# Alternating two accumulation rooms across block boundaries, and a GpSimd power moved one chunk earlier, in a two-layer fp32 network

## The chip, the cores and the metric

The kernel runs on one core of a Trainium2 chip. The metric is the device time of one execution in microseconds (us); lower is better. The kernel before was run three times: 1033.0, 1033.77 and 1033.81 us, median 1033.77.

## The reference, cut to what matters

Two layers follow each other on 2048 rows of 512 numbers. Each layer is an attention and a feed-forward part, and each part is added to its input and layer-normalised. The change lies in the first layer's feed-forward part, whose weights are packed as 4-bit codes with one scale per group of 128 inputs:

```python
w_gu = _dequant_fp4(gate_up_packed, gate_up_scales, 128)   # [2816, 512]
w_down = _dequant_fp4(down_packed, down_scales, 128)       # [512, 1408]
gate_up = jnp.einsum('bsh,oh->bso', x, w_gu)
gate, up = (gate_up[..., :I], gate_up[..., I:])            # I = 1408
h = jax.nn.silu(gate) * up
y = jnp.einsum('bsi,hi->bsh', h, w_down)
rms = jnp.sqrt(jnp.mean(y * y, axis=-1, keepdims=True) + 1e-6)
return y / rms
...
x = _layernorm(x + ffn(x))
```

## The kernel before, in words

**Tiling.** The 2048 rows are four blocks (`NB` = 4) of 512 rows. The hidden width of 1408 is `NI` = 11 chunks of 128. For each block the loop at L625 runs f = 0 to 10; in each pass TensorE computes one chunk of gate and one of up, and the rest of the chip turns them into one chunk of h = silu(gate) * up.

**One chunk.** `scaled_sum` (L452) makes one chunk of gate or of up. For each of the four groups of 128 inputs (k = 0 to 3) TensorE multiplies the unpacked codes with the high and the low part of x (`parts`, the tiles x1Th and x1Tl) into one PSUM bank. The four banks have to be multiplied by their own group scales and added, and that happens in SBUF, in a tile `acc`: for k = 0 ScalarE writes `acc` (L463), for k = 1 to 3 VectorE adds to it (L468; where `by_three` is true the last of them is done by ScalarE and GpSimd, L465 and L466). Banks come from a pool of four (`mm_bank`, L86); chunks with `eight_banks`, which are all of block 0 and f = 9 and 10 of each block, take every second bank from a second pool of four. Then ScalarE applies silu to gate in place (L634) and GpSimd multiplies up and gate into h (L635, called hm in the code).

**The rooms.** `acc` is one of two tiles for gate and one of two for up, allocated at L436 and picked at L454 by `f % 2`. A block has 11 chunks, so f = 10 of one block and f = 0 of the next pick the same room.

**The down projection.** The h of a block is multiplied with the unpacked down weights while the next block's gate and up are made. `down` (L490) is a generator whose steps are single matmuls (L501, L510); the loop takes 5 of them ahead of f = 0 and 8 or 9 after each of f = 0 to 8 (`take`). Its result y lies in one room, `place_w(3, "y")`, which every block uses in turn.

**The work on y.** A finished y is handled one block later still, in blocks 2 and 3 of the loop, by `Normed` (L562): squares of y summed over each row (`squares`, ScalarE, L577, four instructions), the power -0.5 of their mean (`power`, GpSimd, L581 and L582, two instructions on 128x4 numbers), y times that power (`scaled`, ScalarE, L586, four instructions), x + y (`to_x`, GpSimd, L591) and the row statistics and layer norm. `steps` (L600) says after which chunk each of these is issued; L643 calls it.

**Order.** Each engine works through its own queue in order. A planner puts the instructions in that order at build time; it takes an instruction when its inputs are ready by its own reckoning, unless an edge says otherwise. The edges at L636 say that what a pass issues after its chunk comes, on each engine, behind the last gate and up matmul (mm), the last VectorE addition (st), the silu (sl) and the GpSimd product (hm) of that chunk. All waits between engines follow from which instruction reads and writes which tile.

Of the kernel before, what the change touches and what calls it, by code (L numbers as in the profile page):

```python
# [26 lines left out]
NI = I_FF // P  # L27
# [46 lines left out]
def body(ctx: ExitStack, tc: tile.TileContext, a: dict, out: bass.AP):  # L74
# [14 lines left out]
    def acc_bank(name):  # L89
        return pacc.tile([P, 512], F32, tag="acc", name=name)  # L90
# [10 lines left out]
    def place_w(i, name):  # L101
        return wpool.tile([P, KC, C], F32, tag=f"A{i}", name=name)
# [6 lines left out]
    def load_w(dst, name):  # L109
        nc.sync.dma_start(out=dst, in_=a[name].rearrange("(k p) o -> p k o", p=P))  # L110
# [83 lines left out]
    def split_tiles(blk):  # L194

        i, j = ((1, 1), (2, 0), (0, 2), (1, 1))[blk]
        hi = xT_slot(i, "x1Th", F32R)
        lo = wpool.tile([P, KC, 512], F32R, tag=f"A{j}", name="x1Tl")
        return hi, lo

    def split_quarter(parts, blk, i):
        hi, lo = (t[:, :, i * P : (i + 1) * P] for t in parts)
        pt = transposed(x_t[blk][:, i], "x1Tp").rearrange("p (k t) -> p k t", k=KC)
        nc.scalar.copy(hi, pt)  # L204
        nc.vector.tensor_sub(lo, pt, hi.bitcast(F32))
# [66 lines left out]
    for b in range(B):  # L272
        acc = [acc_bank(f"xk{b}_{c}") for c in range(KC)]
# [88 lines left out]
        for n in range(10):  # L362
# [5 lines left out]
            if n >= 1 and n <= 8:  # L368
                i = n - 1
                blk = 2 * b + i // 4  # L370
# [14 lines left out]
            if b == 1 and n in (2, 3, 4, 5):  # L385
                if n == 2:
                    parts = split_tiles(0)
# [23 lines left out]
    def turn(blk, part=range(4)):  # L411

        if 0 in part:
            xT[blk] = xT_tile("x2T")
        for i in part:
            pt = transposed(x_t[blk][:, i], "x2Tp")
            nc.scalar.copy(xT[blk][:, :, i * P : (i + 1) * P], pt.rearrange("p (k t) -> p k t", k=KC))
        return last_turned[0]
# [15 lines left out]
    with tc.tile_pool(name="s2", bufs=1) as wk2:  # L434
        NP = (NI - 1) // 2
        rooms = {n: [wk2.tile([P, 512], F32, name=f"{n}{i}") for i in range(2)] for n in ("gate", "up")}  # L436
# [12 lines left out]
                for j in (slice(0, 3), slice(3, NP)):  # L449
                    yield nc.gpsimd.tensor_sub(dst[:, j], x[:, j], y[:, j])  # L450

        def scaled_sum(f, parts, name, by_three, eight_banks):  # L452

            acc = rooms[name][f % 2]  # L454
            for k in range(KC):
                ps = (acc_bank if eight_banks and k % 2 else mm_bank)(f"{name}p")
                for x in parts:
                    ins = nc.tensor.matmul(  # L458
                        ps, wgu[:, k, f * P : (f + 1) * P], x[:, k], start=x is parts[0], stop=x is parts[1]
                    ).ins  # L460
                s = scale[:, k * FG + f : k * FG + f + 1]
                if k == 0:
                    nc.scalar.activation(acc, ps, AF.Copy, scale=s)  # L463
                elif k == KC - 1 and by_three:
                    nc.scalar.activation(spare, ps, AF.Copy, scale=s)  # L465
                    nc.gpsimd.tensor_add(acc, acc, spare)  # L466
                else:
                    last = nc.vector.scalar_tensor_tensor(acc, ps, s, acc, ALU.mult, ALU.add).ins  # L468
            return acc, ins, last
# [76 lines left out]
        def take(pieces, n):  # L546
            for _ in range(n):
                next(pieces, None)
# [3 lines left out]
        def norm_tiles(blk, mv, part):  # L552

            if blk not in roots:
                rs = roots[blk] = sp.tile([P, 4], F32, tag="rs", name="rs")
                nc.vector.tensor_scalar_add(rs, mv[:, :, 1], 1e-5)
                nc.gpsimd.tensor_tensor(rs, rs, const("mhalf"), ALU.pow)
            for i in part:
                x = x_t[blk][:, i]
                nc.gpsimd.tensor_scalar(x, x, mv[:, i, 0:1], roots[blk][:, i : i + 1], ALU.subtract, ALU.mult)  # L560

        class Normed:  # L562
# [37 lines left out]
            def steps(self):  # L600

                return {
                    0: lambda: self.squares(range(4)),
                    1: lambda: (self.power(), self.scaled(), self.to_x((0, 1))),
                    2: lambda: self.to_x((2, 3)),
                    4: self.stats,
                    5: lambda: self.norm((0,)),
                    7: lambda: self.norm((1,)),
                    8: lambda: self.norm((2, 3)),
                }  # L610
# [12 lines left out]
        for blk in range(NB):  # L623
            h = Hidden(blk)
            for f in range(NI):  # L625
                if f == 0:
                    if blk:
                        with tc.issue_after(mm), tc.issue_after(hm):
                            take(pieces, 5)

                alone = blk == 0 or f >= NI - 2
                gate, mm, st = scaled_sum(f, parts, "gate", False, alone)
                up, mm, st = scaled_sum(NI + f, parts, "up", alone, alone)
                sl = nc.scalar.activation(gate, gate, AF.Silu).ins  # L634
                hm = nc.gpsimd.tensor_mul(h.chunk(f), up, gate).ins  # L635
                with tc.issue_after(mm), tc.issue_after(st), tc.issue_after(hm), tc.issue_after(sl):  # L636
                    if f < NI - 2:
                        take(pieces, 9 if f in (0, NI - 3) else 8)
                    if blk == 0 and f in (2, 4, 6, 8):
                        norm_tiles(3, late, (f // 2 - 1,))  # L640
                    for _ in range((2, 2, 2, 0, 1, 1)[f] if blk == 1 and f < 6 else 0):
                        next(wsums)
                    if blk > 1 and f in old_steps:  # L643
                        old_steps[f]()
                    if f >= NI - 2:
                        if f == NI - 2:
                            if blk < NB - 1:
                                coming = split_tiles(blk + 1)
                            else:
                                Wig = place_w(0, "Wig")  # L650
                                load_w(Wig, "WigT")
                        for i in (0, 1) if f == NI - 2 else (2, 3):
                            if blk < NB - 1:
                                split_quarter(coming, blk + 1, i)
                            else:
                                turn(0, (i,))
            parts = coming
            old, now = now, Normed(blk)
            pieces = down(h, now.room)
            if blk > 0:  # L660
                old_steps = old.steps()
        Wog = place_w(1, "Wog")
        load_w(Wog, "WogT")
        for n, steps in enumerate((11, 12, 10, 12, 10, 10, 14)):
            with tc.issue_after(mm), tc.issue_after(hm):
                take(pieces, steps)
            if n == 0:
                old.squares(range(4))
                old.power()
            if n == 1:  # L670
                for _ in old.rest():
                    pass
            if n < 2:
                turn(1, (2 * n, 2 * n + 1))
            if n == 2:
                lp = logits(0)
# [416 lines left out]
    def finish_ffn(w2, h):  # L1093
# [59 lines left out]
        def steps(b):  # L1153
# [74 lines left out]
            yield  # L1228

        one, two = steps(0), steps(1)  # L1230
        next(one)
        sums_of_h(0, 1)
# [164 lines left out]
```

## Time and profile before

| what | value |
|---|---|
| median of three runs | 1033.77 us |
| the profiled execution: its time, its span | 1033.33 us, 1031.6 us |
| TensorE busy (PE), weight loads (PEld) | 999.9 us (97%), 706.7 us (69%) |
| VectorE (DVE), ScalarE (ACT), GpSimd (POOL) busy | 651.5, 283.9, 306.1 us |
| gate and up of block 0; blocks 1, 2 and 3 begin at about | 255 us; 302, 384 and 471 us |
| mean granted TensorE clock | 0.995 |

The span is the time between the first and the last instruction of the profile; the 1.73 us by which the execution is longer lie around it. [...] idle time of TensorE is read from the gaps between its starts and from the waits, not from the 97%. Weight loads (PEld) run beside the matmuls. In the rows of the timeline, the columns are start and length in us, engine, line, operation, output and inputs, the count of merged instructions, and in square brackets how long the engine was idle before and what released it. In rows of waits the three numbers are us in total, times, and the longest one.

### The profile page before, as it was taken

Reading aid. Unit: us, or ns where it says so; the run is one execution under the profiler, and the core shown is the slowest. Engines: PE = TensorE matmul, PEld = TensorE weight load, DVE = VectorE, ACT = ScalarE, POOL = GpSimd, SP = SyncE. Lnnn points to the kernel's source line nnn. Section 1 sums busy time; section 2 is a strip of 40 time slices with the busy share of each in tenths; the row PEclk is TensorE's granted clock in tenths of the full one; section 3 lists DMA queues with packets and bytes.
Section 4 is the critical chain, followed back from the end, with each engine's and each line's share of the span. In section 5 each row is a group of like instructions: output and inputs, shape, how many; then the busy total and the mean of one; then the engine's idle time right before and its main releaser. Section 6 shows DMA issues by size and latency. Waiting matters only on the chain.

```text
span 1031.6 us, 10932 instructions
## 1 busy us (share of the span) xinstructions
PE 999.9 (97%) x4061; PEld 706.7 (69%) x4061; DVE 651.5 (63%) x1225; ACT 283.9 (28%) x469; POOL 306.1 (30%) x281
## 2 busy tenths in 40 slices
PE   8999999999999998999999999999999999999996
PEld 3454444545767776777778955687687688888885
DVE  1246745376875675675677139446788886689744
ACT  2223232222652244234324043242121123221000
POOL 1100351003785634554556403101005003000022
PEclk9999999999999999999999999999999999999999
DMA  9611123100000000000002050000002422140011
GB/s 346 194 46 56 42 69 98 31 31 0 1 1 1 1 1 0 1 1 1 1 0 93 1 213 1 1 1 1 1 1 82 124 81 82 41 141 24 1 41 41
DMA packets 25688, 48.81 MB, mean 47 GB/s; under 512 B 4652, under 2 KB 6316, under 8 KB 25123
## 3 DMA queue, kind: packets, MB, share of 16 engines
q1 hardware_dynamic: 22995, 42.85, 12.5%
q0 software_dynamic: 1920, 4.22, 1.1%
q10 hardware_dynamic: 720, 1.05, 0.3%
q8 instruction: 32, 0.52, 0.2%
q14 instruction: 21, 0.17, 0.1%
HBM read 39.70 MB, written 10.52 MB: 49 GB/s over the span
## 4 chain that ended last, share of the span: by engine, by line
PE 71%; DVE 10%; issue 9%; ACT 5%; POOL 4%; DMA 0%; POOLq 0%; DVEq 0%; ACTq 0%
PE P L501 11%; PE yp L1141 9%; PE hp L1062 7%; PE qp L210 5%; PE xk L279 5%; PE upp L458 5%; PE ao L210 5%; PE kp L210 4%; DVE gate L468 3%; PE gatep L458 3%; PE ao L945 3%; PE go L901 2%; ACT gate L463 2%; PE kp L296 1%; PE lp L425 1%
## 5 line engine op out<-in xcount | busy, mean ns | idle before, releaser
L468 DVE SCALAR_TENSOR_TENSOR gate<-gatep,scale,gate 128x512 f32<-128x512 f32 x132 | 98.6, 749 | 76.2 <-ACT gate L463 69.8
L174 POOL TENSOR_TENSOR rs<-rs,table 128x4 f32<-128x4 f32 (+1 forms) x21 | 19.6, 936 | 321.2 <-DVE rs L173 320.7
L468 DVE SCALAR_TENSOR_TENSOR up<-upp,scale,up 128x512 f32<-128x512 f32 x115 | 85.9, 747 | 8.1 <-ACT up L463 1.5
L458 PE MATMUL upp<-x1Th,wgu 128*128 128x512 f32 x176 | 75.8, 432 | 10.6 <-ACT gate L463 7.9
L458 PE MATMUL gatep<-x1Th,wgu 128*128 128x512 f32 x176 | 74.5, 430 | 1.2 <-ACT x1Th L204 1.1
L458 PE MATMUL upp<-x1Tl,wgu 128*128 128x512 f32 x176 | 70.5, 403 | 0.0
L458 PE MATMUL gatep<-x1Tl,wgu 128*128 128x512 f32 x176 | 68.6, 399 | 0.1
L635 POOL TENSOR_TENSOR h<-up,gate 128x512 f32<-128x512 f32 x32 | 40.8, 1276 | 87.8 <-DVE up L468 79.7
L501 PE MATMUL P<-wdn,h 128*128 128x256 f32 x256 | 61.9, 379 | 0.0
L458 PEld LDWEIGHTS upp<-x1Th,wgu 128*128 128x128 f32 x176 | 33.6, 191 | 38.2 <-DVE gate L468 18.2
L463 ACT ACTIVATE gate<-gatep,scale 128x512 f32<-128x512 f32 x44 | 30.3, 688 | 104.3 <-PE gatep L458 89.7
L210 PE MATMUL ao<-G,qT 128*128 128x512 f32 x128 | 57.6, 595 | 0.0
L210 PE MATMUL qp<-Wq,x0T 128*128 128x512 f32 x128 | 57.6, 592 | 0.0
L279 PE MATMUL xk<-k,x 128*128 128x512 f32 x128 | 56.7, 592 | 0.0
L945 PE MATMUL ao<-W1o,uT 128*128 128x512 f32 x128 | 55.6, 592 | 0.0
L501 PEld LDWEIGHTS P<-wdn,h 128*128 128x128 f32 x256 | 48.2, 190 | 6.7
L849 POOL TENSOR_TENSOR sum<-sum,sq 128x512 f32<-128x512 f32 x12 | 19.0, 1582 | 107.8 <-issue 84.5
L264 DVE SCALAR_TENSOR_TENSOR k<-kp,e 128x512 f32<-128x512 f32 x16 | 11.0, 691 | 55.4 <-ACT e L263 49.4
L279 PEld LDWEIGHTS xk<-k,x 128*128 128x128 f32 x128 | 24.3, 190 | 30.6 <-issue 29.9
L210 PEld LDWEIGHTS ao<-G,qT 128*128 128x128 f32 x128 | 24.0, 190 | 30.0 <-issue 28.7
L945 PEld LDWEIGHTS ao<-W1o,uT 128*128 128x128 f32 x128 | 24.0, 190 | 28.7 <-issue 28.0
L210 PE MATMUL kp<-Wk,x0T 128*128 128x512 f32 x96 | 43.3, 593 | 0.2 <-DVE k L264 0.2
(335 smaller groups left out, 2131.0 us busy)
## 6 DMA issues: line engine op xcount, KB each, us to landing
pk<-in_gu SPq DMA_DIRECT2D x16, 352.0 KB, 3.8
x<-in_x SPq DMA_DIRECT2D x4, 1024.0 KB, 12.8
w<-in_w SPq DMA_DIRECT2D x1, 4096.0 KB, 14.5
xs<-picked SPq DMA_DIRECT2D x4, 1024.0 KB, 5.0
out<-x SPq DMA_DIRECT2D x4, 1024.0 KB, 4.3
w<-in_w SPq DMA_DIRECT2D x4, 1024.0 KB, 6.4
x0T<-in_xT SPq DMA_DIRECT2D x3, 1024.0 KB, 8.8
pk<-in_dn SPq DMA_DIRECT2D x11, 256.0 KB, 3.5
```

The costliest lines, as they stand in the source:

```text
L174: power = nc.gpsimd.tensor_tensor(rs[:, :n], rs[:, :n], const("mhalf")[:, :n], ALU.pow).ins
L210: nc.tensor.matmul(ps, lhs[:, k], w[:, k], start=start and k == 0, stop=stop and k == KC - 1)
L279: nc.tensor.matmul(acc[c], x_t[2 * b + i // 4][:, i % 4, c * P : (c + 1) * P], k, start=i == 0, stop=i == 7)
L458: ins = nc.tensor.matmul(ps, wgu[:, k, f * P : (f + 1) * P], x[:, k], start=x is parts[0], stop=x is parts[1]).ins
L463: nc.scalar.activation(acc, ps, AF.Copy, scale=s)
L468: last = nc.vector.scalar_tensor_tensor(acc, ps, s, acc, ALU.mult, ALU.add).ins
L501: nc.tensor.matmul(cut, x(j)[:, r], w[:, j], start=j == 0, stop=j == NP - 1 and tail is None)
L635: hm = nc.gpsimd.tensor_mul(h.chunk(f), up, gate).ins
L901: nc.tensor.matmul(ps[:, 256 * m : 256 * m + 256], w[:, k, m], b[:, k, 256 * half : 256 * half + 256], start=k == 0, stop=k == KC - 1,)
L945: nc.tensor.matmul(ao[i], uT[blk][:, k, i * P : (i + 1) * P], W1o[:, k], start=n == 0, stop=n == 3)
L1062: nc.tensor.matmul(ps[:, 256 * j : 256 * j + 256], w[:, k, 2 * g + j], x[:, k], start=k == 0, stop=k == 1)
L1141: nc.tensor.matmul(ps[:, 256 * r : 256 * r + 256], x(r, j), w(j), start=j == 0, stop=j == NJ - 1)
```

## The change

Two edits. First, `scaled_sum` no longer picks its room from f; the caller picks it from the count of chunks over all blocks, `(blk * NI + f) % 2`, the same for gate and up. In block 0 and in block 2 this is the old choice (0 and 22 are even), in blocks 1 and 3 it is the other one. Between f = 10 of a block and f = 0 of the next the room now changes. Nothing else in `scaled_sum` is touched. Second, `power` moves from the step after f = 1 to the step after f = 0, behind `squares`.

```diff
-        def scaled_sum(f, parts, name, by_three, eight_banks):
-
-            acc = rooms[name][f % 2]
+        def scaled_sum(f, parts, acc, name, by_three, eight_banks):
+
             for k in range(KC):
...
-                    0: lambda: self.squares(range(4)),
-                    1: lambda: (self.power(), self.scaled(), self.to_x((0, 1))),
+                    0: lambda: (self.squares(range(4)), self.power()),
+                    1: lambda: (self.scaled(), self.to_x((0, 1))),
                     2: lambda: self.to_x((2, 3)),
...
-                gate, mm, st = scaled_sum(f, parts, "gate", False, alone)
-                up, mm, st = scaled_sum(NI + f, parts, "up", alone, alone)
+                at = (blk * NI + f) % 2
+                gate, mm, st = scaled_sum(f, parts, rooms["gate"][at], "gate", False, alone)
+                up, mm, st = scaled_sum(NI + f, parts, rooms["up"][at], "up", alone, alone)
```

## The prediction, made before the change was run

> **What bounds the kernel now.** I read the page first: the strip of 40 slices, then the shares of the chain that ended last.
>
> ```profile
> PE   8999999999999998999999999999999999999996
> PEclk9999999999999999999999999999999999999999
> ...
> PE 71%; DVE 10%; issue 9%; ACT 5%; POOL 4%; DMA 0%; POOLq 0%; DVEq 0%; ACTq 0%
> ```
>
> TensorE is at work nearly everywhere and carries the chain. So the question is where in the gate and up stage (255 to 560 us) TensorE stands still, and on whom it waits then. The waits of that stretch answer it:
>
> ```profile
> PEld upp L458 <- DVE gate L468: 18.2, 47, 0.9
> PEld upp L458 <- ACT gate L463: 11.3, 8, 3.1
> ...
> ACT y L586 <- POOL ms L582: 9.1, 2, 4.5
> PE upp L458 <- ACT gate L463: 7.9, 8, 2.7
> ```
>
> The first row is a small wait of 47 chunks for a bank, at the pace of VectorE. The second and fourth are the same eight events, few and long: the first up matmul of a chunk waits until ScalarE has written gate and so freed a bank. By the timeline the 7.9 us are twice 2.67 at f = 2 of blocks 2 and 3, 0.89, 0.25 and 0.28 at the three block boundaries, and 1.1 inside block 0, which the change leaves alone. ScalarE in turn waited twice, 4.5 us each, for the power. The chain in order of time shows one of the two, in block 2:
>
> ```profile
> 399.67 1.27 POOL h L635
> 400.94 0.07 issue
> 401.01 0.20 POOL ms L581
> 401.22 0.07 issue
> 401.29 1.04 POOL ms L582
> 402.33 0.02 issue
> 402.36 2.56 ACT y L586 x4
> 404.92 0.58 ACT gate L463
> ...
> 406.33 2.83 PE upp L458 x6
> ```
>
> The product of f = 1, the two power instructions, the four scalings and the gate of f = 2 stand in a row, and TensorE is at its end. Its own timeline says so (bracket: idle before), and the table of windows shows what it does to the clock. The first window is chunk f = 2 of block 1, which has no work on an old y; the second is f = 2 of block 2:
>
> ```profile
> 405.54 0.50 PE L458 MATMUL upp<-x1Th,wgu 128*128 128x512 f32 x1 [2.67 <-ACT gate L463]
> ```
>
> ```profile
> 318.90:326.50 7.60, 7.49 (x33) 5.89 (x32) 4.41 (x6) 2.01 (x3) 4.33 (x4) 1.00 0.01 2
> ...
> 400.70:412.70 12.00, 9.28 (x35) 6.87 (x33) 4.33 (x6) 4.45 (x7) 6.03 (x7) 0.86 0.00 0
> ```
>
> Same matmuls, 12.0 us in place of 7.6, with a granted clock of 0.86 (the number ahead of the two of DMA). The last pair of rows, from the timelines of ScalarE and TensorE, is the boundary between blocks 0 and 1, where the room matters:
>
> ```profile
> 304.41 0.69 ACT L463 ACTIVATE gate<-gatep,scale 128x512 f32<-128x512 f32 x1 [2.73 <-POOL h_even L635]
> ```
>
> ```profile
> 305.15 0.51 PE L458 MATMUL upp<-x1Th,wgu 128*128 128x512 f32 x1 [0.89 <-ACT gate L463]
> ```
>
> Gate of f = 0 waits for the GpSimd product of the old f = 10, which still reads the same room.
>
> [...] after the stall the six up matmuls from 406.33 to 408.95 come every 0.44 us, in a steady chunk every 0.23. [...] 2.67 us without a matmul (3.10 without a weight load) was enough. [...]
>
> **The power, part by part.** Nothing is added; two instructions move up in GpSimd's queue, no DMA and no semaphore of SP is passed. GpSimd's power (0.20 + 1.04 us) now needs the squares of f = 0, which end at 393.5 in block 2; the product of f = 0 ends at 392.9. So it runs from about 393.6 to 394.9. The wait that this adds on GpSimd is 0.7 us; behind it stands only the product of f = 1, whose up is ready at 399.5, so 4.6 us of cover hide it. That hand-over appears at the end of the stage, where power starts 0.08 us after the last squares (601.71 to 601.79).
>
> ScalarE finishes the silu of f = 1 at 397.83, finds the power made, and scales until 400.4 (four at 0.64). Gate of f = 2 is wanted 0.94 us after its first matmul (319.85 against 318.91 in block 1), here at 401.6. So 1.2 us lie between; the stall goes whole. GpSimd's to_x, 2.5 us after the product of f = 1, ends before 403.5, and the next product is due at 407.3 (6.63 after the chunk's start, as in block 1). What is late next in this chunk is the bank wait on VectorE that all chunks have (0.19 + 0.56), and it is within the 7.6.
>
> The gain is the chunk's period. In block 2, first gate matmul of f = 2 to that of f = 3: 412.68 - 400.66 = 12.02; in block 3: 498.81 - 487.05 = 11.76. A steady chunk with the same 8 down matmuls has 7.61 (318.93 to 326.54), and blocks 2 and 3 return to 7.60 at f = 3. Gain 4.41 + 4.15 = 8.56 us. The least is the bare idle time before the matmuls, 2 x 2.67 = 5.3; the rest, 3.2 us, is clock[...]. I take 8.6[...].
>
> **The rooms, part by part.** Block 0 and the inside of each block keep their alternation; f = 0 now takes the room of the old f = 9, whose product ended long ago (300.1 at the first boundary, 380.8 at the second). Gate of f = 0 is then limited by its own matmuls. The weight loads show the high parts of three groups first, then their low parts, the first of which starts at 302.82, 385.21 and 471.56; in a steady chunk ScalarE starts 0.49 us after that matmul (319.36 to 319.85). So gate would start at 303.3, 385.7 and 472.05 instead of 304.41, 386.16 and 472.52. At each boundary I then take the later of two: that bank free 0.72 us on, or TensorE done with the gate matmuls (0.23 after the last start at 303.86, 386.25 and 472.60).
> First: 304.10 instead of 305.15, gain 1.05. Second: 386.48 instead of 386.90, gain 0.42. Third: 472.83 instead of 473.27, gain 0.44. Sum 1.9 us. The later bank waits of that chunk hang on the same gate and up and move along. What is late next is the cast x1Th and subtraction x1Tl, which start the gate matmuls and do not move. The least here is 0, if one of these holds the gate instead; the most is the idle time before the weight loads, 1.3 + 0.69 + 0.7 = 2.7.
>
> **Sum.** 8.56 + 1.91 = 10.5 us. Behind the stage nothing waits for a fixed time: the chain after 560 us is TensorE and loads issued from the same program, so all shifts. The profiled execution took 1033.33 (span 1031.6 and 1.73 around it), so it would take 1022.9; the median of the runs is 0.44 above the profiled one, so 1023.3.
>
> **Rivals.**
> *Only the power pays* (chance 0.13). For: two of three room gains are under half a microsecond, and x1Tl ends just before. 1033.77 - 8.56 = 1025.2.
> *The scalings stay in the way* (0.07). If ScalarE takes them some 2 us later, gate of f = 2 is held for up to 1 us[...]: about 1 + 1 lost, and perhaps part of the clock; 1026 to 1028. For: ScalarE's margin is only 1.2 us. Against: the scalings stand at the same place in the queue as before.
> *The move does not happen* (0.04). The edges only forbid issuing power before the product of f = 0; they do not force it ahead of that of f = 1, so the planner may leave it behind. Only the rooms would pay: 1031.9, no change. Against: the squares end 6 us before that product's inputs.
> *The planner lays out the stage differently* (0.07), the one on the slow side. Its order and its choice of banks follow its own reckoning of times, which both edits alter. If a rotation of banks adds one more wait on VectorE per chunk, as the 0.56 us of the steady chunk, the 27 chunks of f = 0 to 8 in blocks 1 to 3 cost 27 x 0.56 = 15.1, against the 10.5 gained: 1038.4. It decides from 10.5 / 27 = 0.39 us a chunk. For: in f = 9 a gate matmul already stands among the up matmuls (at 367.68), so the planner does shift things. Against: blocks 1, 2 and 3 have the same 7.60 us per chunk with different work beside them.
>
> **How the numbers follow.** Forecast 0.69, the rivals 0.13, 0.07, 0.04 and 0.07 in the order above. The forecast's own range is 1022 to 1025; the first rival falls at its edge and part of the second above. The range 1020.8 to 1027.0 leaves out under 2 in 10, and below holds the larger room gain of 2.7 and some luck in the bank waits. About 0.2% (2.1 us) is what a measurement of this kernel can tell from no change. Faster: 0.69 + 0.13 + 0.07 = 0.89. Within: 0.04. Slower: 0.07.
>
> **What would show it.** Right: ms L582 follows the squares of f = 0 by 0.1 us; no row of ACT y waiting for POOL ms in blocks 2 and 3; f = 2 of both near 7.6 us at a clock of 1.00; ACT gate released by PE gatep at the boundaries; after 560 us the same distances. Wrong: power still behind the product of f = 1; a wait of like length elsewhere in f = 1 to 3; steady chunks no longer 7.60 us; or a gain in the stage that is gone by the end.

## The result and the profile after

| | before | changed |
|---|---|---|
| median of four runs, us | 1033.79 | 1022.03 |
| all runs, us | 1033.0 to 1035.17 | 1021.41 to 1022.87 |
| the profiled execution: time, span, us | 1033.33, 1031.6 | 1022.61, 1020.8 |
| mean granted clock | 0.995 | 0.998 |

The ratio is 0.9885, with a 95% interval of 0.9868 to 0.9903: 1.15% faster. The two profiled executions are 10.7 us apart, the medians 11.8. Line numbers from `scaled_sum` to the loop at L625 are one lower now; silu and the product keep L634 and L635.

The page of the changed kernel, the strip of TensorE and the shares of the chain that ended last:

```profile
PE   8999999999999999999999999999999999999996
...
PE 73%; DVE 10%; issue 8%; ACT 4%; POOL 3%; DMA 0%; POOLq 0%; DVEq 0%; ACTq 0%
```

The slice that read 8, from 387 to 413 us with the first of the two long stalls in it, reads 9, and the chain has two points more of TensorE, less of GpSimd and ScalarE. The waits of the stage (245 to 595 us; us in total, times, longest):

```profile
PEld upp L457 <- DVE gate L467: 18.8, 50, 0.6
...
PEld upp L457 <- ACT gate L462: 3.4, 6, 1.1
...
PE upp L457 <- ACT gate L462: 1.1, 3, 0.6
```

The long waits of up for gate went from 7.9 us in eight to 1.1 us in three, and those three are inside block 0. The row of ACT y behind POOL ms is gone. The many small waits on VectorE stay, 18.8 us after 18.2; the last experiment tests whether they bound the stage now. The timelines of GpSimd and then ScalarE around f = 1 of block 2 show why the long waits went:

```profile
390.14 1.27 POOL L635 TENSOR_TENSOR h<-up,gate 128x512 f32<-128x512 f32 x1 [1.64 <-DVE up L467]
392.12 0.20 POOL L580 TENSOR_SCALAR ms<-ms 128x4 f32<-128x4 f32 x1 [0.70 <-ACT rw L576]
392.39 1.03 POOL L581 TENSOR_TENSOR ms<-ms,table 128x4 f32<-128x4 f32 x1
```

```profile
395.82 0.63 ACT L634 ACTIVATE gate<-gate 128x512 f32<-128x512 f32 x1 [0.72 <-DVE gate L467]
396.36 2.54 ACT L585 ACTIVATE y<-y,ms 128x512 f32<-128x512 f32 x4
400.14 0.69 ACT L462 ACTIVATE gate<-gatep,scale 128x512 f32<-128x512 f32 x1 [1.23 <-PE gatep L457]
```

The power follows the squares of f = 0 and is ready at 393.4, three microseconds before ScalarE asks for it. The scalings follow the silu without a gap, and then ScalarE waits 1.23 us for TensorE, no longer the other way round. The windows of chunk f = 2, in block 1 and then in blocks 2 and 3 (length, five busy times, granted clock, DMA share, GB/s):

```profile
317.85:325.45 7.60, 7.49 (x34) 5.89 (x33) 4.41 (x6) 2.01 (x3) 4.33 (x4) 1.00 0.01 2
399.30:406.80 7.50, 7.41 (x34) 5.88 (x33) 4.41 (x6) 2.01 (x3) 3.74 (x4) 1.00 0.00 0
480.60:488.10 7.50, 7.41 (x35) 5.88 (x33) 4.41 (x6) 2.01 (x3) 3.73 (x4) 1.00 0.00 1
```

What took 12.0 us at a clock of 0.86 takes 7.5 at 1.00. At the first boundary, ScalarE and then TensorE:

```profile
303.29 0.69 ACT L462 ACTIVATE gate<-gatep,scale 128x512 f32<-128x512 f32 x1 [1.73 <-PE gatep L457]
```

```profile
304.03 0.50 PE L457 MATMUL upp<-x1Th,wgu 128*128 128x512 f32 x1
```

Gate of f = 0 is released by its own matmuls, and the first up matmul has no wait in brackets any more; only its weight load still waits 0.34 us for gate, at each of the three boundaries.

Read from the first gate matmul of each chunk, the stage (f = 0 of block 0 to f = 10 of block 3) took 301.95 us before and 291.40 after, a gain of 10.55:

| part | before, us | after, us | gain |
|---|---|---|---|
| f = 0 of blocks 1, 2, 3 | 9.66, 8.75, 8.78 | 8.66, 8.40, 8.41 | 1.00 + 0.35 + 0.37 |
| f = 2 of blocks 2, 3 | 12.02, 11.76 | 7.54, 7.54 | 4.48 + 4.22 |
| f = 4 of block 2 | 7.95 | 7.61 | 0.34 |
| f = 1 of blocks 1, 2, 3 | 7.54, 7.54, 7.54 | 7.59, 7.59, 7.60 | -0.17 |
| all other chunks | | | -0.04 |

From there to the end both take 482.19 us; the other 0.17 us between the two profiles lie ahead of the stage.

The orders of the two programs' instructions are equal on TensorE, ScalarE and SP. On GpSimd the power has changed places with the product of f = 1, twice. On VectorE the planner has made one more change of its own: in f = 2 of blocks 2 and 3 it placed gate, gate, up, gate, up, up before, and gate three times and up three times now. A kernel below has the new order and the old stalls.

### The profile page after: what moved, and what is told of

It reads as the page before. It is cut to its first block, busy times and chain, and to the rows that moved or that the text cites. A ratio compares the mean times of both kernels' runs of the same rounds, so it can differ in the third digit from the quotient of the medians.

```text
span 1020.8 us, 10937 instructions
## 1 busy us (share of the span) xinstructions
PE 996.1 (98%) x4061; PEld 704.8 (69%) x4061; DVE 651.7 (64%) x1225; ACT 284.1 (28%) x469; POOL 306.4 (30%) x281
## 3 DMA queue, kind: packets, MB, share of 16 engines
q0 software_dynamic: 1920, 4.22, 1.1%
## 4 chain that ended last, share of the span: by engine, by line
PE 73%; DVE 10%; issue 8%; ACT 4%; POOL 3%; DMA 0%; POOLq 0%; DVEq 0%; ACTq 0%
PE P L500 11%; PE yp L1141 9%; PE hp L1062 7%; PE qp L210 5%; PE xk L279 5%; PE upp L457 5%; PE ao L210 5%; PE kp L210 4%; DVE gate L467 4%; PE gatep L457 4%; PE ao L945 3%; PE go L901 2%; ACT gate L462 2%; PE kp L296 1%; PE lp L425 1%
## 5 line engine op out<-in xcount | busy, mean ns | idle before, releaser
L635 POOL TENSOR_TENSOR h<-up,gate 128x512 f32<-128x512 f32 x32 | 40.9, 1278 | 77.4 <-DVE up L467 59.6
L457 PEld LDWEIGHTS upp<-x1Th,wgu 128*128 128x128 f32 x176 | 33.0, 187 | 29.9 <-DVE gate L467 18.8
```

The costliest lines, as they stand in the source:

```text
L457: ins = nc.tensor.matmul(ps, wgu[:, k, f * P : (f + 1) * P], x[:, k], start=x is parts[0], stop=x is parts[1]).ins
```

## The experiments

Each kernel is the changed one with the edit shown. The kernel before ran beside them on the same chip, and the ratios are to it. Lengths of chunks are read from the first gate matmul to the next chunk's.

**The power alone.**

```diff
-                at = (blk * NI + f) % 2
+                at = f % 2
```

> The power early, the rooms as before (f % 2). Theory A (two independent stalls that add up): f = 2 of blocks 2 and 3 takes about 7.55 us as in the changed kernel, the three boundaries keep their waits; 8.6 to 8.8 us faster than before, so about 1.8 us slower than the changed kernel, near 1024 to 1025. Rival B (the rooms' gain is only lent, since TensorE meets the next bank wait anyway): no slower than the changed kernel, about 1022. Rival C (the rooms are what pays): about 1031.

Measured: 1023.94 us against 1033.44 before, ratio 0.9904 (0.9888 to 0.9921). f = 2 of blocks 2 and 3 takes 7.53 us each, and the boundaries are those of the kernel before. Its timeline of ScalarE at the first one:

```profile
304.41 0.69 ACT L462 ACTIVATE gate<-gatep,scale 128x512 f32<-128x512 f32 x1 [2.71 <-POOL h_even L635]
```

The old wait for the product of f = 10 is back, 2.71 us after 2.73. So 9.5 us come with the power alone, and the rest needs the rooms. In the profile its stage is 9.0 us shorter than before: 8.7 in f = 2 and 0.35 in f = 4 of block 2.

**The rooms alone.**

```diff
-                    0: lambda: (self.squares(range(4)), self.power()),
-                    1: lambda: (self.scaled(), self.to_x((0, 1))),
+                    0: lambda: self.squares(range(4)),
+                    1: lambda: (self.power(), self.scaled(), self.to_x((0, 1))),
```

> The rooms by the count over all blocks, the power after f = 1 as before. Theory A: the boundaries gain 1.0 + 0.4 + 0.4 = 1.8 us and f = 2 of blocks 2 and 3 still takes about 12 us; 1.8 us faster than before, near 1032. Rival B: no faster than before, 1033.8. Rival C: about 1024.

Measured: 1031.74 against 1033.44, ratio 0.9982 (0.9974 to 0.9991), 1.7 us. The windows of f = 2 in blocks 2 and 3:

```profile
399.00:411.40 12.40, 9.68 (x35) 7.01 (x34) 4.32 (x6) 4.46 (x7) 6.82 (x8) 0.86 0.00 0
485.50:497.50 12.00, 9.30 (x35) 7.04 (x33) 4.32 (x6) 4.45 (x7) 5.93 (x7) 0.86 0.00 1
```

Both stalls are there with the low clock. The boundaries take 8.67, 8.41 and 8.42 us, as in the changed kernel. In the profile the stage is only 0.9 us shorter than before, since these two chunks are 0.31 and 0.23 us longer than there. 9.5 + 1.7 = 11.2 us for the parts stands against 11.8 for the whole, within what the intervals allow: the two gains add up. Rivals B and C fall.

**The power late, the scalings later still.** If the harm is the place of the scalings in ScalarE's queue, a late power does no harm when they too are late.

```diff
-                    0: lambda: (self.squares(range(4)), self.power()),
-                    1: lambda: (self.scaled(), self.to_x((0, 1))),
-                    2: lambda: self.to_x((2, 3)),
+                    0: lambda: self.squares(range(4)),
+                    1: self.power,
+                    2: lambda: (self.scaled(), self.to_x(range(4))),
```

> The rooms as changed; the power as late as before (behind the product of f = 1), but the four scalings and all of to_x one chunk later, after f = 2. Theory A (the harm is that gate of f = 2 stands behind the scalings in ScalarE's queue, not that the power is late): no stall in f = 2, as fast as the changed kernel within 1 us, though the copy into y at f = 3 may wait 0.5 to 1 us for to_x, which nobody on TensorE waits for. Rival D (the late power itself, or the late to_x, holds something else up, the room y or a bank of the down projection): slower than the changed kernel by 2 us or more, with a wait of TensorE or of the copy into y at f = 3.

Measured: 1022.41 us, ratio 0.9894 (0.9878 to 0.9911), the same as the changed kernel. ScalarE in block 2:

```profile
403.47 2.54 ACT L585 ACTIVATE y<-y,ms 128x512 f32<-128x512 f32 x4
407.31 0.69 ACT L462 ACTIVATE gate<-gatep,scale 128x512 f32<-128x512 f32 x1 [1.29 <-PE gatep L457]
...
411.69 0.59 ACT L523 COPY y<-P 128x512 f32<-128x512 f32 x1 [0.54 <-POOL x L590]
```

The scalings now stand in the gap of f = 2, and gate of f = 3 still has 1.29 us to spare. The copy into y waits 0.54 us for to_x, as expected, and nobody for it. So the power behind the product of f = 1 was harmless in itself; only what waited for it in front of gate was not. Rival D falls.

**Gate's rooms alone.**

```diff
-                up, mm, st = scaled_sum(NI + f, parts, rooms["up"][at], "up", alone, alone)
+                up, mm, st = scaled_sum(NI + f, parts, rooms["up"][f % 2], "up", alone, alone)
```

> The power early; the gate rooms by the count over all blocks, the up rooms as before (f % 2). Theory A (gate is written first and the first up bank waits on gate alone; up of f = 0 is written 1.5 us later, when the product of the old f = 10 has ended): as fast as the changed kernel within 0.4 us. Rival E (up's room waits as well): about 1 us slower than the changed kernel, with ScalarE's up of f = 0 released by the product of f = 10.

Measured: 1022.62 us, ratio 0.9896 (0.9879 to 0.9912). Up of f = 0 at the first boundary, on ScalarE:

```profile
303.97 0.69 ACT L462 ACTIVATE up<-upp,scale 128x512 f32<-128x512 f32 x1 [0.89 <-PE upp L457]
```

It shares its room with the old f = 10 again and yet waits for TensorE, since the product is over by then (303.34). The stage takes 291.50 us after 291.40. Only gate's room mattered; rival E falls.

**The power delayed step by step.** Four kernels put n more powers ahead of it, with n = 2, 4, 5 and 6, to measure the cover and the price of a stall. The sums of squares are unchanged, since what is added to them is multiplied with 0. Where the expectations say that TensorE cools, they mean that its granted clock falls.

```diff
+            def late(self, n):
+                t = sp.tile([P, 4], F32, tag="late", name="late", bufs=1)
+                nc.gpsimd.tensor_copy(t, self.ms)
+                for _ in range(n):
+                    nc.gpsimd.tensor_tensor(t, t, const("mhalf"), ALU.pow)
+                nc.gpsimd.tensor_scalar(t, t, 0.0, 0.0, ALU.mult, ALU.add)
+                nc.gpsimd.tensor_add(self.ms, self.ms, t)
...
-                    0: lambda: (self.squares(range(4)), self.power()),
+                    0: lambda: (self.squares(range(4)), self.late(n), self.power()),
```

> The changed kernel with the power made late on purpose: ahead of it on GpSimd a copy, two more powers on a spare tile, a product with 0 and an addition to the sums of squares, some 3 us by the 1.03 us of one power. Theory A (cover of 2.9 us until ScalarE has done the silu of f = 1, and 1.2 us more until gate of f = 2 is wanted): nothing on TensorE, f = 2 of blocks 2 and 3 stays at 7.55 us at a clock of 1.00, span as the changed kernel's 1020.8 within 0.7. Rival F (there is no such cover, each delay of the power costs): 2 x 3 = 6 us slower.

> As the one before with four powers, some 5.2 us late. Theory A: gate of f = 2 comes 1 us late, TensorE stands 0.7 us in each of the two chunks, with the clock at 1.00: span about 1.5 us over the changed kernel's. Rival F: 10 us over. Rival G (each stall of TensorE cools it, however short): 1.5 us and 3 us of clock, 4 to 5 us over.

> As before with five powers, some 6.3 us late. Theory A: TensorE stands 1.8 us in each of the two chunks; if cooling needs more than that, the clock stays at 1.00 and the span is about 3.6 us over the changed kernel's. Rival G: 6.5 us over, with a clock of about 0.86 in f = 2.

> As before with six powers, some 7.4 us late. Theory A: TensorE stands 2.9 us in each of the two chunks, as long as in the kernel before, and cools as there: a granted clock near 0.86 in f = 2, 2 x (2.9 + 1.5) = 9 us over the changed kernel's span. Rival H (the clock fell in the kernel before for another reason, such as VectorE's order in f = 2): the clock stays at 1.00 and the span is 6 us over.

Each ran once. Spans: 1020.8, 1021.3, 1026.1 and 1029.5 us, against 1020.8 of the changed kernel. The start of the stage moves by up to 1.3 us between profiles, so the chunk f = 2 itself says more (first gate matmul to that of f = 3):

| powers added | f = 2, blocks 2 and 3, us | TensorE's idle time before up | granted clock |
|---|---|---|---|
| 2 | 7.53, 7.53 | none | 1.00, 1.00 |
| 4 | 8.47, 8.50 | 0.32, 0.36 | 1.00, 1.00 |
| 5 | 9.55, 11.20 | 1.40, 1.45 | 1.00, 0.85 |
| 6 | 12.26, 12.05 | 2.50, 2.54 | 0.86, 0.86 |

Two powers cost nothing, so the cover is real and rival F falls. With four, gate of f = 2 starts at 399.83 by ScalarE's timeline where the first gate matmul at 398.03 would have let it start 0.86 us on: it is 0.94 late, and the chunk is 0.94 us longer, though TensorE's own row shows only 0.32 us of idle time. The rest comes back in the waits of up's weight loads for VectorE, which adds to gate later: 1.0 us in this chunk, 0.5 in the changed kernel. With five in block 2 it is 2.02 late by the same reckoning (401.67 against 398.79), and the chunk 2.02 longer. So in these two chunks, at a clock of 1.00, the delay of gate cost its whole length.

Five powers also separate the clock from the stall, within one run. The up matmuls of blocks 2 and 3, by TensorE's timeline:

```profile
402.39 0.50 PE L457 MATMUL upp<-x1Th,wgu 128*128 128x512 f32 x1 [1.40 <-ACT gate L462]
```

```profile
485.63 0.51 PE L457 MATMUL upp<-x1Th,wgu 128*128 128x512 f32 x1 [1.45 <-ACT gate L462]
```

The two stalls are nearly the same, and yet the windows of the two chunks read:

```profile
398.80:408.30 9.50, 7.92 (x33) 5.77 (x32) 4.41 (x6) 4.45 (x7) 5.05 (x5) 1.00 0.00 0
482.00:493.20 11.20, 9.58 (x35) 7.02 (x33) 4.41 (x6) 4.45 (x7) 6.76 (x7) 0.85 0.00 1
```

The slow clock made 11.20 - 9.55 = 1.65 us there. Rival G (every stall lowers the clock) falls with four powers, whose 0.32 and 0.36 us left it at 1.00, but theory A, which left open one length of stall from which the clock falls, is too simple: after 1.45 us it fell and after 1.40 it did not. Narrower windows show what differs. In block 3 the clock is one half from 487.30 to 490.71, for 3.41 us. The last two rows below are that stretch and the 3.41 us ahead of it. The first two are the same length before and after 401.97, which is 85.33 us ahead of 487.30, the distance that two such stretches have in other runs (measured below). The first number after the length is TensorE's busy time:

```profile
398.56:401.97 3.41, 2.42 (x11) 1.68 (x9) 0.00 (x0) 2.77 (x5) 3.41 (x4) 1.00 0.00 0
401.97:405.38 3.41, 2.82 (x10) 1.73 (x11) 2.80 (x4) 1.57 (x3) 0.93 (x1) 1.00 0.00 0
...
483.89:487.30 3.41, 1.79 (x7) 0.62 (x5) 1.50 (x2) 2.38 (x4) 2.26 (x2) 1.00 0.00 0
487.30:490.71 3.41, 3.41 (x8) 2.75 (x9) 2.91 (x4) 0.63 (x1) 0.12 (x1) 0.50 0.01 2
```

The stall of block 3 lies whole in the 3.41 us ahead of the half-rate stretch, in which TensorE was busy for 1.79 us; that of block 2 is split at 401.97, and its two windows were busy for 2.42 and 2.82. The other stretches are compared below.

With six powers VectorE's order in f = 2 is that of the changed kernel and the clock falls all the same, so rival H (VectorE's order lowers the clock) falls. The chunks are as long as in the kernel before, 12.26 and 12.05 us after 12.02 and 11.76, so the new order is not where the gain comes from either.

**What bounds the stage then.** The small waits on VectorE are left. TensorE could do two down steps while VectorE adds up gate (a step is one matmul of the program and two rows in the trace, which start 0.216 us apart). The second kernel takes four instead of two.

```diff
                 gate, mm, st = scaled_sum(f, parts, rooms["gate"][at], "gate", False, alone)
+                if f < NI - 2:
+                    with tc.issue_after(mm), tc.issue_after(st):
+                        take(pieces, 2)
...
-                        take(pieces, 9 if f in (0, NI - 3) else 8)
+                        take(pieces, (9 if f in (0, NI - 3) else 8) - 2)
```

> The changed kernel with two of the 8 or 9 down steps of a chunk moved between its gate and its up matmuls (f = 0 to 8). This is about what bounds the stage once the long stalls are gone: a steady chunk takes 7.60 us where its 16 matmuls of 0.2335 and 16 of 0.216 us need 7.19, and TensorE waits 0.20 + 0.56 us for VectorE to free gate's banks. Theory (the wait is only a matter of order; two steps, 0.86 us, cover it): the steady chunk falls to about 7.2 us, 27 x 0.4 = 11 us faster than the changed kernel, near 1011. Rival (VectorE or the bank count is the bound, so the wait comes back as a wait of up's last bank or of the next gate): no faster than the changed kernel by more than 3 us.

> The same with four steps moved, half of them. Theory: as with two, about 1011, since two steps cover the wait already. Rival: with four steps up comes 1.7 us later and its banks are not free for the next gate, so it is slower than with two steps by some 0.3 us a chunk, near 1019.

Measured: 1010.6 us with two steps, ratio 0.9781 (0.9767 to 0.9796), and 1015.95 with four, 0.9835 (0.9819 to 0.9850). With two steps, the page's chain, a window of one chunk of block 1, and the small wait on VectorE:

```profile
PE 77%; issue 8%; DVE 7%; POOL 3%; ACT 3%; DMA 0%; POOLq 0%; DVEq 0%; ACTq 0%
```

```profile
316.40:323.60 7.20, 7.20 (x34) 6.04 (x33) 4.50 (x6) 1.90 (x3) 4.35 (x4) 1.00 0.01 2
```

```profile
PEld upp L457 <- DVE gate L467: 1.1, 5, 0.4
```

The steady chunk takes 7.18 us by its starts (316.44 to 323.62), which is the 7.19 that the distances of its matmuls add up to (16 of 0.2335 us and 16 of 0.216), and the stage 279.96 us after 291.40. The small wait fell from 18.8 to 1.1 us, so it was what bounded the stage, and it was a matter of order; the planner also moved some instructions on VectorE, ScalarE and GpSimd, which was not tested apart. This is faster than both kernels, by 11.4 us than the changed one's median.

Four steps give 5.3 us of it back. The theory (about 1011) missed this, and the rival (near 1019) had it in the wrong place: most chunks stay at 7.17. The steps that read other engines' work come too early. TensorE in f = 3 of block 1, and ScalarE in f = 3 of block 2:

```profile
328.76 0.70 PE L500 MATMUL P<-T,h 128*128 128x256 f32 x2 [1.79 <-POOL T L450]
```

```profile
410.40 0.59 ACT L523 COPY y<-P 128x512 f32<-128x512 f32 x1 [4.39 <-POOL x L590]
```

The first waits for GpSimd's sums of the down weights, and that chunk takes 10.86 us at a clock of 0.84. The second is a copy into y, which now stands ahead of silu and up in ScalarE's queue and waits until to_x has read the old y; f = 3 and f = 4 of blocks 2 and 3 take 7.7 to 8.2 us.

## Why the prediction was right

1023.3 us was forecast, 1020.8 to 1027.0 the range; 1022.03 was measured. Point by point:

- **The power.** The mechanism held. 8.56 us were forecast, 4.48 + 4.22 = 8.70 seen. The wait that it adds on GpSimd is 0.70 us as forecast; ScalarE's margin before gate of f = 2 is 1.23 us, forecast 1.2. That the clock stays at 1.00 without the stall held in both chunks. The kernel with the power alone measures 9.5 us; f = 2 accounts for 8.7 there too and f = 4 of block 2 for 0.35, and the remainder lies within its interval.
- **Its least value was mis-sized.** The lower end, 2 x 2.67 = 5.3 us, took TensorE's idle time before the up matmuls as the stall and the other 3.2 us as clock. The runs with four and five powers show that the chunk loses gate's whole delay. Gate of f = 2 in block 2 followed the scalings at about 404.8 instead of 401.5, 3.3 us late; that leaves 1.1 of the 4.4 us for the clock. The same working on all seven stalls after which the clock fell (two each in the kernel before, with the rooms alone and with six powers, one with five) leaves 0.9 to 1.6 us. The sum did not suffer, because it came from the lengths of whole chunks.
- **The rooms.** 1.91 us were forecast, 1.00 + 0.35 + 0.37 = 1.72 seen in the profile, of which f = 1 gives back 0.17, with the rooms alone too. That the medians with the rooms alone differ by 1.7 is in part luck, since the profiled stages there differ by 0.9. Gate starts 1.68 us after the first gate matmul of f = 0 (303.29 after 301.61), where 303.3 after 301.73 was worked out, 1.57. The three gains came out 0.05 to 0.07 us lower each. That TensorE's next wait moves along held; that up's room takes no part was not said, and holds.
- **The rest of the program.** After the stage nothing changes (482.19 us in both). The planner kept TensorE's order, so the rival on the slow side has no ground here. The small wait on VectorE that the prediction gives to 47 chunks is 47 waits in 28 chunks; nothing in its sum rests on that.
- **The 1.3 us beyond the forecast.** The profiled executions are 10.7 us apart, where 10.5 was forecast. 0.34 us of that is f = 4 of block 2, which took 7.95 us before and 7.96 with the rooms alone, and 7.54 to 7.61 in the changed kernel, its other three parts and the four delayed ones. It goes with VectorE's new order in f = 2 and not with the early power: with six powers the stall is back and f = 4 takes 7.59. How that order reaches f = 4 was not found. The remaining 1 us lies between the median of the runs and the profiled one, which the four runs of each do not settle: the ratio's interval stands for a gain of 10.0 to 13.6 us, and 10.5 is in it. The kernel before also varies with its clock. Of its 18 runs beside the first four experiments, the three with a mean clock of 0.997 took 1030.8 to 1030.9 us and the five with 0.992 took 1033.7 to 1034.7, while all four runs of the changed kernel have 0.998. The author's estimate is that the number of half-rate stretches, and with it what the two stalls cost, differs from one execution to the next: 3.41 us at a clock of 0.50 take 0.0017 off the mean of an execution of 1031 us, and the means differ by 0.005. The forecast rested on one profile.

On the clock the runs show the following. Each half-rate stretch of this stage lasts 3.41 us, at 0.50. The two of one execution start at 406.47 and 491.80 in the kernel before, at 405.79 and 491.13 with the rooms alone and at 404.92 and 490.25 with six powers: 85.33 or 85.34 us apart each time, which is 25 times 3.41 us to within 0.1, though the stalls themselves are 86.4, 86.4 and 85.9 us apart. In the 3.41 us ahead of each of these stretches, of the one with five powers and of the one with four steps TensorE was not idle throughout but busy for 0.73 to 1.79 us; in the kernel before, whose 2.67 us without a matmul the prediction found enough, for 0.87 us both times. When the stage is divided into 25ths of that distance, counted from the starts of the stretches, TensorE was busy for 2.31 us or more in all other parts, and the clock stayed at 1.00. Between 1.79 and 2.31 us nothing was measured, and why the stretches stand at that distance was not shown.

## What to carry to other kernels

When an engine's queue holds work that is urgent behind work that is not, look at what the second kind waits for: a GpSimd power of 1.03 us cost 8.7 us here because four patient scalings that needed it stood ahead of gate, the one urgent read of a bank. Moving the power earlier or the scalings later cured it. Count such a stall by the length of the whole stretch against an undisturbed twin, not by the idle time on the row of the engine that suffers, since part of it came back here in later waits (0.94 us of delay with 0.32 us of idle time) and in the clock (1.65 us with five powers). When alternating buffers meet an odd number of passes, let the count run on across the outer loop; and once long waits are gone, see whether the small regular ones are only a matter of order, as they were here (18.8 us fell to 1.1).

## What was not expected of the hardware

A stall of TensorE of 1.40 us left the clock at 1.00, and after one of 1.45 us in the same execution it was at one half for 3.41 us, which cost 1.65 us. In the 3.41 us ahead of that stretch TensorE had been busy for 1.79 us; in the two windows of that length which share the stall of 1.40 us it was busy for 2.42 and 2.82. After stalls of 2.5 to 2.7 us the clock fell each time in these profiles (two each in the kernel before, with the rooms alone and with six powers), and so it did after the one of 1.79 us with four steps. So in these runs the length of a stall alone does not tell whether the clock falls. What does was not shown; the busy times above are what differed.
